# First attention: softmax rows transposed by VectorE in 32x32 blocks and a trip through DRAM, values a step later

## The chip, the core and the metric

The kernel runs on one core of a Trainium2 chip. A core has engines that work side by side, each through its own queue in order: TensorE (PE: matrix products and transposes), VectorE (DVE), ScalarE (ACT), GpSimd (POOL), and SyncE (SP), which only issues transfers (DMA). A transfer can also be issued from ScalarE's and GpSimd's queues. The engines share an on-chip memory, SBUF, of 128 partitions; TensorE writes to PSUM, which is used in banks of 128x512 float32. An instruction that waits for a semaphore holds back everything behind it on its own queue. The metric is the device time of one execution in microseconds (us).

## The reference

Four residual layers on x of 4 batches x 512 rows x 512 columns, float32, each behind a layer norm: a first attention, a feed-forward with ternary weights, a second attention with block-scaled weights, and the same feed-forward again. The change lies in the first attention and in work that runs beside it. That attention has 16 query heads over 4 key/value heads of 128, and adds causal softmax attention with rotary positions to a gated linear attention:

```python
scores = jnp.einsum('bqhd,bkhd->bhqk', sq, sk) * scale
scores = jnp.where(causal[None, None], scores, jnp.finfo(scores.dtype).min)
attn = jax.nn.softmax(scores, axis=-1)
y = jnp.einsum('bhqk,bkhd->bqhd', attn, sv)
o = 0.5 * y + 0.5 * o_gla
return o.reshape(b, n, H * D) @ Wo
```

`o_gla` is a recurrence over the rows with decays from the keys. The kernel computes it by chunks of 128 rows: products within a chunk (`own`) plus a state carried from the chunks before.

## The kernel before

**Tiling.** A group is one batch and one key/value head with its four query heads; there are 16 groups. Each has four chunks of 128 query rows, so 64 chunks. For chunk c of its group the scores reach over the c+1 chunks of keys up to its own, so their width is 128, 256, 384 or 512.

**The loop** in `first_attention_gentle` (from L518) runs over steps n, one chunk a step, and is pipelined over chunks by hand: a step works on the later parts of an early chunk and the early parts of a later one. The parts of a chunk are methods of `Chunk`:

- A projects its queries (L181 through `project`) and copies them to `q_t` (ScalarE, L430).
- B makes `qd`, softmax over the head dimension times a decay (L328 to L334: VectorE and ScalarE), and `qr`, the rotation (L319 and L322 on VectorE, the swapped half `sw` on GpSimd, L321).
- C transposes `qr` and `qd` on TensorE (L340) through a PSUM bank `tp`.
- own makes the chunk's part of the linear attention, masked by `until` (L448, L450).
- D(h) takes the scores of one head (TensorE, L456), adds the mask, takes the maximum (L459), exponentials with their sum (ScalarE, L462), reciprocal (L463) and the division (VectorE, L464). The result is `pr`, with query rows on the partitions.
- E(j) transposes key chunk j of the four heads' `pr` on TensorE (L472), four transposes to a bank, and takes the bank to SBUF as `wts`: for the chunk's own keys with `own` added (VectorE, L475), else by a copy on ScalarE (L477).
- F multiplies the values with `wts`, and the carried state with `qdT` (L484, L486), and halves the sum (`oT`, L488).
- G multiplies by Wo and adds to the residual (L181, L186).

In step n the chunk n+1 runs own and D, chunk n runs E between these and then F, chunk n-1 runs G, chunk n+2 runs C, chunk n+3 A and B. `part` prepares the next group: project, gates, decays (the running sum of the gates by a product with `until_r`, halves `gatehi` and `gatelo`), transposes of `kr` and `kd`, states.

**Beside it** two generators advance once a step. `quantise` makes the ternary weights of the feed-forward and stores them to DRAM as `blocks`. `prepare` multiplies codes by scales of the second attention's weights for 64 slices: five loads from SP a slice (L274, L276), a product on GpSimd (L290), a rounding copy on ScalarE (L281), a comparison on VectorE that counts inexact entries (L282), a store from SP to `exact` (L283).

**What sets the order.** The kernel's program order is the start of it; a scheduler then places instructions on each engine's queue by their dependences, except that those wrapped in `in_place` keep their order among each other. Buffers by tag (`bufs`) and PSUM banks (mm 2, sc 3, tp 2, pv 1) set what must wait for a reader.

**Feed-forward.** `feed_forward` keeps 11 weight blocks in SBUF (`block`, L252), in pools that take the place of the attention's. Block 0 is loaded into the pool `base` during the first attention (step 58) and serves both feed-forwards.

Of the kernel before, what the change touches and what calls it, by code (L numbers as in the profile page):

```python
# [19 lines left out]
P = 128  # L20
# [4 lines left out]
HG = 4  # L25
# [49 lines left out]
def hybrid_block(ctx: ExitStack, tc: tile.TileContext, a: dict, out: bass.AP):  # L75
# [186 lines left out]
    def prepare(pool):  # L262
# [5 lines left out]
        def fetch(i):  # L268
            g, n, k = slices[i]
            name = ("wq", "wk", "wv", "wo")[n]  # L270
            codes, scales = a[f"{name}_codes"], a[f"{name}_scales"]
            r, cols = (g * NK + k, slice(0, C)) if n == 3 else (k, slice(g * HG * D, (g + 1) * HG * D))
            w, sc = tiles[i] = [pool.tile([P, C], F32, tag=x, name=x) for x in ("codes", "scales")]
            in_place(nc.sync.dma_start(w, codes[r * P : (r + 1) * P, cols]))  # L274
            for q in range(4):
                in_place(nc.sync.dma_start(sc[q * 32 : (q + 1) * 32], scales[r * 4 + q, cols].partition_broadcast(32)))  # L276

        def rounded(i):
            g, n, k = slices[i]
            w, to = tiles.pop(i)  # L280
            in_place(nc.scalar.copy(to.bitcast(F32R), w))  # L281
            in_place(nc.vector.scalar_tensor_tensor(w, w, 1.0, to, ALU.mult, ALU.not_equal, accum_out=inexact[:, i : i + 1]))  # L282
            in_place(nc.sync.dma_start(exact[g, n, :, k, :], to))  # L283

        for i in range(-2, len(slices)):
            if i >= 0:
                rounded(i)
            if 0 <= i + 1 < len(slices):
                w, sc = tiles[i + 1]
                in_place(nc.gpsimd.tensor_tensor(w, w, sc, ALU.mult))  # L290
            if i + 2 < len(slices):
                fetch(i + 2)
# [3 lines left out]
    def first_attention_gentle(base, extra):  # L296

# [3 lines left out]
        with ExitStack() as st:  # L301
# [6 lines left out]
            until = one.tile([P, P], F32, tag="until", name="until")  # L308
            nc.scalar.dma_start(until, a["sums"][:, PREFIX, :])
            until_r = one.tile([P, P], F32R, tag="until_r", name="until_r")  # L310
            nc.scalar.copy(until_r, until)
# [38 lines left out]
            class Group:  # L350
# [33 lines left out]
                def decays(self):  # L384
# [4 lines left out]
                    project(dec.rearrange("p c d -> p (c d)"), lambda i: until_r, lambda i: halves[i].rearrange("p c d -> p (c d)"), 2)  # L389
# [7 lines left out]
                    self.kr = one.tile([P, NC, D], F32, tag="kr", name="kr")  # L397
# [24 lines left out]
            class Chunk:  # L422
# [9 lines left out]
                def B(self):  # L432
# [3 lines left out]
                    self.qr = two.tile([P, HG, D], F32, tag="qr", name="qr")  # L436
                    rotate(self.qr, self.q_t, turn[:, c : c + 1, 0:1, :], turn[:, c : c + 1, 1:3, :])

                def C(self):
                    self.qrT = two.tile([P, HG, P], F32, tag="qrT", name="qrT")  # L440
                    transposed(self.qrT, self.qr, nc.scalar.copy)
                    self.qdT = two.tile([P, HG, P], F32, tag="qdT", name="qdT", bufs=3)
                    transposed(self.qdT, self.qd, nc.scalar.copy)

                def own(self):
# [4 lines left out]
                    nc.vector.tensor_tensor(self.own_, sc, until.unsqueeze(1).to_broadcast([P, HG, P]), ALU.mult)  # L450
                    self.prs, self.wts = [], []

                def D(self, h):
                    c, width = self.c, (self.c + 1) * P
                    sc = bank("sc", [P, width])
                    nc.tensor.matmul(sc, lhsT=self.qrT[:, h, :], rhs=self.k.krT[:, :width], start=True, stop=True)  # L456
                    nc.vector.tensor_tensor(sc[:, c * P :], sc[:, c * P :], causal, ALU.add)
                    nm = two.tile([P, 1], F32, tag="nm", name="nm", bufs=4)
                    nc.vector.tensor_reduce(nm, sc, AX.X, ALU.max, negate=True)  # L459
                    pr = two.tile([P, S], F32, tag="pr", name="pr", bufs=7)[:, :width]  # L460
                    den = two.tile([P, 1], F32, tag="den", name="den", bufs=4)
                    nc.scalar.activation(pr, sc, AF.Exp, bias=nm, accum_out=den)  # L462
                    nc.vector.reciprocal(den, den)  # L463
                    nc.vector.tensor_scalar(pr, pr, den, None, ALU.mult)  # L464
                    self.prs.append(pr)

                def E(self, j):
                    if j > self.c:
                        return
                    tp = bank("tp", [P, HG, P])  # L470
                    for h in range(HG):
                        nc.tensor.transpose(tp[:, h, :], self.prs[h][:, j * P : (j + 1) * P], ident)  # L472
                    w = two.tile([P, HG, P], F32, tag="wts", name="wts", bufs=5)
                    if j == self.c:
                        nc.vector.tensor_tensor(w, self.own_, tp, ALU.add)  # L475
                    else:
                        nc.scalar.copy(w, tp)  # L477
                    self.wts.append(w)

                def F(self):  # L480
                    c = self.c
                    acc = bank("pv", [P, HG, P])
                    if c:
                        nc.tensor.matmul(acc, lhsT=self.k.state[:, c - 1, :], rhs=self.qdT, start=True, stop=False)  # L484
                    for j in range(c + 1):
                        nc.tensor.matmul(acc, lhsT=self.k.v_t[:, j, :], rhs=self.wts[j], start=j == c == 0, stop=j == c)  # L486
# [31 lines left out]
            for n in range(-7, last + 1):  # L518
# [4 lines left out]
                if p == 3 and (m + 1) % KV == 0 and (m + 1) // KV < B:  # L523
                    normalise((m + 1) // KV)
                part(m, p, 0)
                w, x, y, z = (at(i) for i in range(4))
                if n == -6:
                    nc.scalar.dma_start(turn, a["turn"])
                if x:
                    x.own()  # L530
                if w:
                    w.E(0)
                if x:
                    x.D(0)
                if w:
                    w.E(1)
                if z and n > -2:
                    z.A()
                if w:
                    w.E(2)  # L540
                if x:
                    x.D(1)
                if w:
                    w.E(3)
# [4 lines left out]
                if y:  # L549
                    y.C()  # L550
                if x:
                    x.D(3)
                part(m, p, 1)
# [567 lines left out]
```

## Time and profile before

Times are those of three runs: 2556.14, 2558.22 and 2559.29 us, median 2558.22. The profile is one further execution.

| what | value |
|---|---|
| the profiled execution | 2560.28 us |
| its span, first to last instruction | 2558.5 us |
| granted TensorE clock, mean | 0.998 |
| busy over the span: PE / DVE / ACT / POOL | 2523.9 / 1676.9 / 1140.8 / 248.4 us |
| first attention | to 1127 us |
| first feed-forward | 1127 us to about 1380 |
| second attention | about 1380 to 2306 us |
| last feed-forward | from 2306 us |
| moved by DMA | 248.88 MB, mean 97 GB/s |

A row of the groups reads: line, engine, operation, output<-input, the shapes, how many, then busy us and mean ns of one, then the idle time of the engine just before them and what ended it. Busy us counts overlapped time once, so with pipelined matrix products the mean times the count is more than the busy time. A float32 product of 128x512 counts as two MATMUL instructions; a transpose as one. In the chain of waits each piece begins where the one before it ended, so its lengths add up to the span. Bounds of stages come from the chain; the stretches of the busy table were cut by hand.

### The profile page before, as it was taken

Reading aid. Unit: us, or ns where it says so; the run is one execution under the profiler, and the core shown is the slowest. Engines: PE = TensorE matmul, PEld = TensorE weight load, DVE = VectorE, ACT = ScalarE, POOL = GpSimd, SP = SyncE. Lnnn points to the kernel's source line nnn. Section 1 sums busy time; section 2 is a strip of 40 time slices with the busy share of each in tenths; the row PEclk is TensorE's granted clock in tenths of the full one; section 3 lists DMA queues with packets and bytes.
Section 4 is the critical chain, followed back from the end, with each engine's and each line's share of the span. In section 5 each row is a group of like instructions: output and inputs, shape, how many; then the busy total and the mean of one; then the engine's idle time right before and its main releaser. Section 6 shows DMA issues by size and latency. Waiting matters only on the chain.

```text
span 2558.5 us, 29656 instructions
## 1 busy us (share of the span) xinstructions
PE 2523.9 (99%) x9448; PEld 1633.4 (64%) x9448; DVE 1676.9 (66%) x3858; ACT 1140.8 (45%) x2901; POOL 248.4 (10%) x263
## 2 busy tenths in 40 slices
PE   7999999999999999999999999999999999999999
PEld 5555555555555555568887666666666666657887
DVE  6888777888788878754445666666766666664332
ACT  4555555555555555542223444444444444432222
POOL 2121112112221121200001000000000000000000
PEclk9999999999999999999999999999999999999999
DMA  4344433443343332250003334353444434333000
GB/s 125 91 128 131 129 101 115 145 135 96 103 128 111 101 114 66 83 184 23 1 1 102 95 94 124 94 142 91 124 108 111 124 93 124 94 68 136 17 17 22
DMA packets 159045, 248.88 MB, mean 97 GB/s; under 512 B 33952, under 2 KB 61984, under 8 KB 154784
## 3 DMA queue, kind: packets, MB, share of 16 engines
q1 hardware_dynamic: 157584, 245.50, 33.4%
q8 instruction: 77, 1.26, 0.2%
q10 hardware_dynamic: 1296, 1.39, 0.2%
q14 instruction: 88, 0.72, 0.1%
HBM read 150.03 MB, written 29.62 MB: 70 GB/s over the span
## 4 chain that ended last, share of the span: by engine, by line
PE 90%; DVE 6%; DMA 2%; SPq 1%; issue 1%; ACT 0%; POOL 0%; ACTq 0%; DVEq 0%
PE mm L181 43%; PE sc L181 12%; PE sc L821 8%; PE sc L456 5%; PE pv L486 4%; PE tp L855 4%; PE pv L855 4%; PE tp L472 3%; PE tp L340 2%; PE sc L448 2%; PE pv L484 1%; PE tp L160 1%; SPq L848 1%; DVE qd L334 1%; DVE qr L319 1%
## 5 line engine op out<-in xcount | busy, mean ns | idle before, releaser
L826 ACT ACTIVATE pr<-sc,nm 128x512 f32<-128x512 f32 x256 | 175.9, 687 | 322.4 <-DVE nm L823 277.6
L181 PE MATMUL sc<-xnhi,block 128*128 128x512 f32 x704 | 278.7, 396 | 2.5 <-DMA block<-blocks 2.5
L181 PE MATMUL sc<-xnlo,block 128*128 128x512 f32 x704 | 275.6, 392 | 0.0
L821 PE MATMUL sc<-kT,qT 128*128 128x512 f32 x512 | 262.2, 594 | 0.0
L181 PE MATMUL mm<-xnhi,w 128*128 128x512 f32 x512 | 254.5, 497 | 0.0
L181 PE MATMUL mm<-wq,xnT 128*128 128x512 f32 x512 | 232.2, 595 | 0.0
L181 PE MATMUL mm<-wo,oT 128*128 128x512 f32 x512 | 231.4, 593 | 0.0
L823 DVE TENSOR_REDUCE nm<-sc 128x1 f32<-128x512 f32 x256 | 175.1, 684 | 82.0 <-PE sc L821 79.6
L462 ACT ACTIVATE pr<-sc,nm 128x128 f32<-128x128 f32 (+3 forms) x256 | 133.9, 523 | 162.7 <-DVE nm L459 157.7
L181 PE MATMUL mm<-xnlo,w 128*128 128x512 f32 x512 | 206.0, 402 | 0.0
L843 DVE STREAM_TRANSPOSE turned<-pr 128x512 f32<-128x512 f32 x256 | 173.5, 696 | 33.4 <-ACT pr L833 30.0
L833 ACT ACTIVATE pr<-pr,den 128x512 f32<-128x512 f32 x192 | 138.6, 722 | 79.3 <-DVE den L831 79.1
L456 PE MATMUL sc<-krT,qrT 128*128 128x512 f32 (+3 forms) x512 | 172.3, 434 | 0.0
L181 PEld LDWEIGHTS mm<-wo,oT 128*128 128x128 f32 x512 | 96.7, 190 | 118.0 <-issue 117.7
L321 POOL TENSOR_TENSOR sw<-q_t,turn 128x256 f32<-128x256 f32 x128 | 94.7, 760 | 676.5 <-ACT q_t L430 616.6
L1022 DVE TENSOR_TENSOR hT<-hT,sc 128x512 f32<-128x512 f32 x88 | 60.5, 687 | 141.0 <-PE sc L181 137.9
L181 PEld LDWEIGHTS mm<-wq,xnT 128*128 128x128 f32 x512 | 94.1, 192 | 91.4 <-issue 90.1
L181 PEld LDWEIGHTS sc<-xnhi,block 128*128 128x128 f32 x704 | 132.8, 189 | 30.7 <-issue 3.6
L181 PEld LDWEIGHTS sc<-xnlo,block 128*128 128x128 f32 x704 | 133.0, 189 | 27.3 <-issue 0.5
L486 PE MATMUL pv<-wts,v_t 128*128 128x512 f32 x320 | 147.9, 593 | 0.0
L821 PEld LDWEIGHTS sc<-kT,qT 128*128 128x128 f32 x512 | 95.7, 189 | 80.5 <-issue 63.1
L186 DVE TENSOR_TENSOR x<-x,mm 128x512 f32<-128x512 f32 x128 | 87.4, 684 | 78.6 <-PE mm L181 76.9
(143 smaller groups left out, 4968.0 us busy)
## 6 DMA issues: line engine op xcount, KB each, us to landing
prT<-turned SPq DMA_DIRECT2D x1024, 64.0 KB, 2.0
w<-exact SPq DMA_DIRECT2D x32, 1024.0 KB, 5.4
wq<-in_Wq SPq DMA_DIRECT2D x16, 1024.0 KB, 5.3
wo<-in_Wo SPq DMA_DIRECT2D x16, 1024.0 KB, 5.8
exact<-scales SPq DMA_DIRECT2D x64, 256.0 KB, 3.1
block<-blocks SPq DMA_DIRECT2D x21, 512.0 KB, 7.8
w<-in_w3T SPq DMA_DIRECT2D x22, 256.0 KB, 4.7
block<-blocks SPq DMA_DIRECT2D x21, 256.0 KB, 7.8
```

The lines of the kernel that those rows point to most:

```text
L181: nc.tensor.matmul(acc, lhsT=lhs(k), rhs=rhs(k), start=k == 0, stop=k == n - 1)
L186: nc.vector.tensor_tensor(xs[b * NC + c], xs[b * NC + c], y, ALU.add)
L321: nc.gpsimd.tensor_tensor(sw[:, :, i, :], s4[:, :, 1 - i, :], sin[:, :, i, :].to_broadcast([P, n, D // 2]), ALU.mult)
L456: nc.tensor.matmul(sc, lhsT=self.qrT[:, h, :], rhs=self.k.krT[:, :width], start=True, stop=True)
L462: nc.scalar.activation(pr, sc, AF.Exp, bias=nm, accum_out=den)
L486: nc.tensor.matmul(acc, lhsT=self.k.v_t[:, j, :], rhs=self.wts[j], start=j == c == 0, stop=j == c)
L821: nc.tensor.matmul(sc, lhsT=qTs[u][:, i * P : (i + 1) * P], rhs=kTs[u], start=True, stop=True)
L823: nc.vector.tensor_reduce(nm, sc, AX.X, ALU.max, negate=True)
L826: nc.scalar.activation(pr, sc, AF.Exp, bias=nm, accum_out=den)
L833: nc.scalar.mul(pr, pr, den)
L843: nc.vector.transpose(turns[u][:, :, i, :], pr.rearrange("p (q k) -> p q k", q=4))
L855: nc.tensor.matmul(accs[u].rearrange("p (n t) -> p n t", t=32), lhsT=v_ts[m, j][:, h * D : (h + 1) * D], rhs=prTs[u].rearrange("p a i (k t ...
```

## The change

Softmax rows no longer go through TensorE. D divides on ScalarE, and VectorE transposes the result in 32x32 blocks into one tile `turned` for the four heads; after the last head one transfer stores it to DRAM (`passed`), and E becomes four loads, one for each 32 partitions of `prT`, which bring the blocks to their places. So that this gives a whole transpose, the keys of the scores are taken in an order with the block index outermost (the rearranged `krT`), and the mask is read in the same order.

```diff
-    nc.tensor.matmul(sc, lhsT=self.qrT[:, h, :], rhs=self.k.krT[:, :width], start=True, stop=True)
+    nc.tensor.matmul(sc.rearrange("p q (k j) -> p q k j", j=32), lhsT=self.qrT[:, h, :], rhs=self.k.krT.rearrange("p (k q j) -> p q k j", q=4, j=32)[:, :, :n, :], start=True, stop=True)
...
     nc.vector.reciprocal(den, den)
-    nc.vector.tensor_scalar(pr, pr, den, None, ALU.mult)
-    self.prs.append(pr)
+    nc.scalar.mul(pr, pr, den)
+    nc.vector.transpose(self.turned.rearrange("p (q h x) -> p q h x", q=4, h=HG)[:, :, h, :], pr.rearrange("p (q x) -> p q x", q=4))
+    if h == HG - 1:
+        self.passed = dram.tile([P, 4 * HG * P], F32, tag="passed", name="passed", bufs=3)[:, : 4 * HG * 32 * n]
+        in_place(nc.sync.dma_start(self.passed, self.turned))
...
-    tp = bank("tp", [P, HG, P])
-    for h in range(HG):
-        nc.tensor.transpose(tp[:, h, :], self.prs[h][:, j * P : (j + 1) * P], ident)
-    w = two.tile([P, HG, P], F32, tag="wts", name="wts", bufs=5)
-    if j == self.c:
-        nc.vector.tensor_tensor(w, self.own_, tp, ALU.add)
-    else:
-        nc.scalar.copy(w, tp)
+    prT = two.tile([P, HG * P * (3 + self.c % 2)], F32, tag=f"prT{self.c % 2}", name="prT", bufs=1)[:, : 4 * HG * 32 * n]
+    for q in range(4):
+        in_place(nc.sync.dma_start(prT[32 * q : 32 * (q + 1)].rearrange("j (a x) -> j a x", a=4), self.passed.rearrange("(a j) (q x) -> q j a x", a=4, q=4)[q]))
+    self.wts = prT.rearrange("p (a h k t) -> p h a k t", a=4, h=HG, t=32)
```

F adds `own` to the last key chunk of `prT` on VectorE and multiplies from views of `prT`:

```diff
+    w = self.wts[:, :, :, c, :]
+    nc.vector.tensor_tensor(w, w, self.own_.rearrange("p h (a t) -> p h a t", a=4), ALU.add)
...
-        nc.tensor.matmul(acc, lhsT=self.k.v_t[:, j, :], rhs=self.wts[j], start=j == c == 0, stop=j == c)
+        nc.tensor.matmul(acc.rearrange("p h (a t) -> p h a t", a=4), lhsT=self.k.v_t[:, j, :], rhs=self.wts[:, :, :, j, :], start=j == c == 0, stop=j == c)
```

The loop runs one step further. F and G of a chunk come one step later, own a step later, C moves from late in the step to its start:

```diff
-            for n in range(-7, last + 1):
+            for n in range(-7, last + 2):
...
+                u, v, w, x, y, z = (at(i) for i in range(-2, 4))
+                if n >= -1:
+                    next(prepared, None)
+                if w:
+                    w.E()
                 part(m, p, 0)
...
+                if y:
+                    y.C()
                 if x:
                     x.D(0)
                 if z and n > -2:
                     z.A()
                 if x:
                     x.D(1)
+                if v:
+                    v.F()
+                if n >= -1:
+                    next(prepared, None)
                 if z:
                     z.B()
                 if x:
                     x.D(2)
+                if w:
+                    w.own()
...
+                part(m, p, 1)
+                if u:
+                    u.G()
+                if x:
+                    x.D(3)
```

`prepare` advances twice a step; its transfers are issued by GpSimd, and the inexact entries are found by a subtraction on GpSimd and an absolute sum on ScalarE in place of VectorE's comparison:

```diff
-            in_place(nc.sync.dma_start(w, codes[r * P : (r + 1) * P, cols]))
+            in_place(nc.gpsimd.dma_start(w, codes[r * P : (r + 1) * P, cols]))
             for q in range(4):
-                in_place(nc.sync.dma_start(sc[q * 32 : (q + 1) * 32], scales[r * 4 + q, cols].partition_broadcast(32)))
+                in_place(nc.gpsimd.dma_start(sc[q * 32 : (q + 1) * 32], scales[r * 4 + q, cols].partition_broadcast(32)))
...
+            in_place(nc.gpsimd.tensor_tensor(w, w, to, ALU.mult))
             in_place(nc.scalar.copy(to.bitcast(F32R), w))
-            in_place(nc.vector.scalar_tensor_tensor(w, w, 1.0, to, ALU.mult, ALU.not_equal, accum_out=inexact[:, i : i + 1]))
-            in_place(nc.sync.dma_start(exact[g, n, :, k, :], to))
+            in_place(nc.gpsimd.tensor_tensor(w, w, to, ALU.subtract))
+            in_place(nc.scalar.activation(w, w, AF.Abs, accum_out=inexact[:, i : i + 1]))
+            in_place(nc.gpsimd.dma_start(exact[g, n, :, k, :], to))
```

To fit in SBUF some tiles share or lose buffers: `kr` takes the tag of `gate`, `qr` has one buffer in place of two, `pr` three in place of seven, `qdT` four in place of three; `until` is kept once, in the rounded type, and filled by GpSimd at step -6. Block 0 of the feed-forward is no longer kept in `base`:

```diff
-        early = ahead(50, 0)
-        early.setdefault(58, []).extend(lambda f=f: heads.append(block((base, base), f)) for f in range(1))
-        first_attention_gentle(base, early)
+        first_attention_gentle(base, ahead(50, 0))
...
-            ws = ws + [block(pools, f) for f in range(len(ws), NF)]
+            ws = [block(pools, f) for f in range(NF)]
```

## The prediction

> **What bounds the kernel now.** I read the busy times by stage first, because the page's line 1 averages over four stages.
>
> ```profile
> core 0: us, PE busy (x) PEld busy (x) DVE busy (x) ACT busy (x) POOL busy (x), PEclk, DMA share, GB/s
> ...
> 256.00:384.00 128.00, 127.93 (x467) 73.77 (x466) 100.66 (x256) 67.80 (x210) 25.14 (x26) 1.00 0.37 115
> ...
> 640.00:768.00 128.00, 127.08 (x482) 73.69 (x481) 106.27 (x299) 68.36 (x210) 27.77 (x30) 1.00 0.38 115
> ```
>
> In the first attention (0 to 1127 us) TensorE is busy over 99% of each stretch at full clock; VectorE is at about 81%, ScalarE at 53%, GpSimd at 20%. TensorE sets the time, so an edit gains what it takes from TensorE's queue and loses what TensorE then waits for. Next the groups by form between 128 and 1024 us (columns: line, engine, operation, output<-input, shapes, count | busy us, mean ns | idle before).
>
> ```profile
> L472 PE MATMUL tp<-ident,pr 128*128 128x128 f32 x520 | 78.0, 273 | 0.0
> L321 POOL TENSOR_TENSOR sw<-q_t,turn 128x256 f32<-128x256 f32 x103 | 76.1, 759 | 554.4 <-ACT q_t L430 494.5 <-DVE pr L464 47.8 <-DVE mv L132 12.1
> L290 POOL TENSOR_TENSOR codes<-codes,scales 128x512 f32<-128x512 f32 x52 | 75.1, 1444 | 99.5 <-DMA scales<-in_wv_scales 19.8 <-DVE pr L464 19.1 <-DMA scales<-in_wo_scales 15.4
> L319 DVE TENSOR_TENSOR qr<-q_t,turn 128x512 f32<-128x512 f32 x52 | 49.8, 957 | 0.0
> L477 ACT COPY wts<-tp 128x512 f32<-128x512 f32 x78 | 44.7, 580 | 22.2 <-PE tp L472 22.1
> L282 DVE SCALAR_TENSOR_TENSOR codes<-codes,scales 128x512 f32<-128x512 f32 x52 | 37.0, 711 | 0.0
> L475 DVE TENSOR_TENSOR wts<-own,tp 128x512 f32<-128x512 f32 x52 | 35.3, 679 | 22.8 <-PE tp L472 22.8
> L464 DVE TENSOR_SCALAR pr<-pr,den 128x384 f32<-128x384 f32 x52 | 27.2, 522 | 1.3
> L464 DVE TENSOR_SCALAR pr<-pr,den 128x512 f32<-128x512 f32 x52 | 24.8, 477 | 0.5
> L319 DVE TENSOR_TENSOR kr<-k_t,turn 128x512 f32<-128x512 f32 x13 | 8.7, 666 | 0.0
> ```
>
> The transposes of L472 are what the change removes. Their mean of 273 ns is not their price, since they are pipelined; the chain of waits gives the time between them. The same view gives the stage boundaries:
>
> ```profile
> 1091.57 0.44 PE tp L472 x4
> ...
> 1127.65 3.91 DMA block<-blocks
> ```
> ```profile
> 2306.48 3.76 DMA block<-blocks
> ```
>
> So 0.109 us per transpose. The x16 runs of projections in that chain stand at 220.99, 288.77 and 356.75 us: 67.9 us per group of four chunks, 17.0 us per step of the loop.
>
> **The change part by part.**
>
> *TensorE.* Per group E made (1+2+3+4) x 4 = 40 transposes; over 16 groups 640 x 0.109 = **69.5 us leave the bound engine**, and a step falls from 17.0 to 15.9 us. No product is added. The products now read their moving operand in runs of 32; the second attention does that already (L855, mean 593 ns, as L486 has with whole rows), so I cost it at nothing.
>
> *VectorE.* Gone: L464 in four widths (296+383+522+477 ns) x 64 = 107; L475, 64 x 0.68 = 43; the check of L282 with its 81 ns accumulator read, 64 x 0.79 = 51; together 201 us. Added: 256 block transposes and 64 additions of `own`. For the transposes two rows of the second attention stand near:
>
> ```profile
> L843 DVE STREAM_TRANSPOSE turned<-pr 128x512 f32<-128x512 f32 x256 | 173.5, 696 | 33.4 <-ACT pr L833 30.0 <-DMA prT<-turned 3.0
> L833 ACT ACTIVATE pr<-pr,den 128x512 f32<-128x512 f32 x192 | 138.6, 722 | 79.3 <-DVE den L831 79.1
> ```
>
> L459 over the same widths takes 284/410/551/680 ns; a transpose at 696 is 16 more, so (300+426+567+696) x 64 = 127. The addition has both inputs in SBUF: between 666 ns (the `kr` row) and 957 (the `qr` row); I take 0.8, 51 us. Net -23 us: it stays near 83% of a shorter stage.
>
> *ScalarE.* Gone: 96 copies x 0.58 = 56. Added: the division, 722 ns at 512 and less by the steps of L462 (360/476/578/678), so (404+520+622+722) x 64 = 145; and `Abs` with its accumulator read, near 629+193 ns (L380, L396), 53. Net +142 us: from about 53% to 70%. Hidden as long as no TensorE wait ends on it.
>
> *GpSimd.* Today a step holds 2 x 0.76 + 0.4 (`sw` of q, and of k spread) + 1.44 = 3.4 us. Added: a subtraction (1.44, as L290) and six DMA issues. No row shows an issue from GpSimd. From below: an issue by SP, 0.44 us (four `scales` took 1.77 us in the timeline). From above: the Trainium skill (DMA: Bandwidth & Descriptors, Anatomy of one DMA) counts about 2.0 us fixed for a whole DMA of this kind, of which the issue can be only a part. I take 1.0 us, the first-byte latency that the same page gives under Latency and other measured facts, where it puts it down to this issuing work; an estimate. The step then has 10.8 us of 15.9 (7.4 to 16.8 by the two ends).
>
> Here a rule speaks against the change. SBUF — State Buffer (Who interferes with whom) says that VectorE with two SBUF inputs, and GpSimd reading SBUF, lock one another out for a whole instruction. The row first:
>
> ```profile
> 388.42 1.27 POOL L290 TENSOR_TENSOR codes<-codes,scales 128x512 f32<-128x512 f32 x1
> ...
> 388.60 1.64 DVE L319 TENSOR_TENSOR qr<-q_t,turn 128x512 f32<-128x512 f32 x1
> ```
>
> L319 took 1.64 us beside GpSimd against 0.67 for the `kr` form: the trace agrees. By the rule at its worst each of the 64 subtractions costs VectorE its whole 1.44, 92 us, and VectorE would stand at 92%. By the rows, the excess of L319 and L322 (957 and 882 over 666) is 64 x 0.51 = 32 us for 212 us of GpSimd arithmetic; 92 us more adds 14. I take 14. The same section warns that descriptors written by GpSimd wait for VectorE in a two-port mode; L464, whose 512 form is faster than its 384 form and so may run in one, leaves VectorE, which weakens that.
>
> *The DMA path.* A chunk's `turned` goes to DRAM and back before F. Rows near:
>
> ```profile
> w<-exact SPq DMA_DIRECT2D x32, 1024.0 KB, 5.4
> ...
> exact<-scales SPq DMA_DIRECT2D x64, 256.0 KB, 3.1
> ```
>
> At most 1 MB out (5.4), four issues of 0.44 to 0.59, 256 KB in (3 to 5): 12 us. Before it VectorE finishes the last head (4 to 8 us). In the built order the TensorE work from the last score of a chunk to the product needing its weights is about 24 us, so it is hidden with 4 us or more to spare. On SP the store waits for VectorE, and the loads behind it for its landing; `wq` (5.3 us) and `wo` (5.8) stand behind such waits. In the order `wq` comes before the loads of its step and has a step to land; `wo` is issued when its last reader ends and has 14 us. Both hidden; a late one costs its excess, once a group.
>
> *C earlier, F later.* In the built order the TensorE work between a chunk's q projection (A) and the transposes of its q (C) falls from about 17 us to 9.3-12.4. The chain between is q_t 0.59, maximum 0.68, four exponentials with reads 2.3, reciprocal 0.17, four L334 1.5: 5.3 us, and some 7 us as VectorE's queue stands. Slack shrinks to about 2 us at the tightest step. `sw`, which `qr` needs, stands on GpSimd behind the issues; in one step of four (second chunk, values late) the chain subtraction, six issues, product ends about 2.4 us after q_t is there. Also the projection of k to the gates' product has 4.3 us of TensorE work in place of 6.9, for a chain of 0.27+1.09+0.63+0.63+0.68+0.62 = 3.9 plus five handovers. These two are **what is late next**: I put 1.1 us a group on the two together at each of 16 groups, 18 us (5 to 35).
>
> *Block 0.* It was resident at both feed-forwards and gave 16 products (3.6 us) while block 1 came. Now block 0 itself is loaded only when the last product has freed its place: the two DMA lines above (3.91, 3.76), bare. Less the 0.5 waited today at the first, **+7.4 us**.
>
> *Ends.* The extra step at the end of the loop leaves the last round trip less cover: about 16 us of path against 19 us of TensorE work in the order; +3 (0 to 8). At the start ScalarE no longer waits for `until` (11.30 us), worth up to 2 us, but the gates' product stands with less ahead of it: +1.
>
> **Sum**: -69.5 + 7.4 + 3 + 1 + 18 = -40 on a span of 2558.5: 2518. The profiled execution took 2560.3 and the runs' median is 2558.2, so the span stands for the median: **2518 us**.
>
> **The rivals.**
> 1. *All slack holds* (no late q, no late gates): 2500. For it: by the waits of TensorE up to 1150 us no cause but the first layer norm (12.2 us) holds it for more than 2.0 us in all. Against: those distances are cut by a third. Chance 0.12.
> 2. *GpSimd becomes the bound* (the other side). At 2 us an issue its step is 16.8 us, with about 1 us of waiting for ScalarE's copy before the subtraction 17.8, and `sw` then holds `qr`: 64 x 0.8 = +51, with the ends +11: **2620**. It decides from 1.85 us an issue, (15.9 - 4.8)/6; slower than now from about 1.9. Against: 4.8 us of the step is arithmetic, and the price I took leaves 5 us free. Chance 0.17.
> 3. *VectorE's queue becomes the bound*: a transpose behind a reciprocal waits for ScalarE's division. In the order about half stand directly behind it, 8 x 0.7 = 5.5 us a group on 53 of 63.6: enough room. If all wait and the port lock is at its worst, 53 + 11 + 5 = 69 us a group, 1 more than now; halfway, 66, the gain shrinks to about 12-20 us: 2542. Chance 0.13.
> 4. *The weights come late*: a miss of 5 us a group, 80 us, on the main sum: 2590. Chance 0.05.
>
> **How the numbers follow.** The forecast itself has 0.53, with a range of its own of 2503 to 2540. Two runs of this kernel differ by about 3 us (2556.14 to 2559.29), so 0.2%, 5 us, is no change. Faster: 0.53 + 0.12 + most of rival 3, 0.10 = 0.75. Same: 0.04. Slower: 0.17 + 0.05 less the edge = 0.21. Below 2490 nothing leads; to leave out no more than 0.2 the range goes up to 2582.
>
> **What would show it.** No `tp<-pr` rows before 1100 us; TensorE at 96% or more in the stage and groups 64 to 65 us apart; waits of PE ending on `qr`, `qd` or `gatehi`, a few tenths to 2 us each; bare waits on block 0 near 4 us twice; GpSimd's issues near 1 us and `sw` late one step in four. I am wrong if `sw` is late in every step, if PE waits on `prT`, or if groups stay 68 us apart.

## The result, and the profile after

The changed kernel takes 2646.45 us (median of 4 runs, 2641.98 to 2649.09) against 2558.34 before (4 runs, 2556.14 to 2559.29): a ratio of 1.0344, interval 1.0326 to 1.0362. It is slower by 88 us; the forecast was 2518. The profiled execution has a span of 2643.5 us and a mean granted clock of 0.981 (before: 2558.5 and 0.998).

The windows of the changed kernel, the same two stretches as before and then the whole first attention:

```profile
core 0: us, PE busy (x) PEld busy (x) DVE busy (x) ACT busy (x) POOL busy (x), PEclk, DMA share, GB/s
256.00:384.00 128.00, 121.23 (x393) 65.77 (x391) 101.35 (x242) 79.29 (x242) 58.03 (x78) 1.00 0.69 195
640.00:768.00 128.00, 116.84 (x365) 64.95 (x364) 96.16 (x225) 76.24 (x228) 52.83 (x74) 0.95 0.57 165
0.00:1206.92 1206.92, 1084.70 (x3470) 593.06 (x3470) 928.31 (x2245) 715.92 (x2137) 497.79 (x687) 0.96 0.59 172
```

No engine is the bound any more: in the two stretches TensorE fell from over 99% to 95% and 91%, VectorE is no fuller, ScalarE and GpSimd have room. The chain of waits gives the ends of the stages:

```profile
1206.92 3.58 DMA block<-blocks
...
2389.76 3.65 DMA block<-blocks
```

The first attention ends at 1206.92 us instead of 1127.65, 79.3 later; what follows takes 1436.6 us (2643.5 less 1206.92) instead of 1430.9. These 5.7 us are put down to block 0, and the loss lies in the first attention. The same window of the kernel before:

```profile
0.00:1127.65 1127.65, 1105.78 (x4088) 639.82 (x4089) 892.14 (x2359) 597.60 (x1846) 218.78 (x238) 1.00 0.37 111
```

TensorE is busy for 1084.70 us, against 1105.78 before: 21 less. It is idle for 122.2 us (1206.92 less 1084.70), against 21.9: 100 more. The two make the 79. What it waits for, from TensorE's waits in that stretch (line, releaser, us in total, times, longest), and below it the gates' wait in the kernel before:

```profile
PE mm L181 <- ACT gatehi L120: 57.4, 15, 6.2
PE tp L160 <- DVE xn L157: 24.2, 9, 8.5
PE mm L181 <- DVE x L186: 7.6, 8, 1.6
PE mm L181 <- ACT v_t L378: 7.0, 6, 1.8
...
PE pv L493 <- DVE prT L488: 2.3, 6, 0.6
```
```profile
PE mm L181 <- ACT gatehi L120: 2.0, 3, 1.2
```

The gates' product waits in 15 of the 16 groups, 3.8 us on average. The way through DRAM (`prT`) costs next to nothing. One such wait by windows of 2 us:

```profile
382.00:384.00 2.00, 0.37 (x1) 0.00 (x0) 1.06 (x3) 2.00 (x8) 1.42 (x3) 1.00 0.45 145
384.00:386.00 2.00, 0.00 (x0) 0.00 (x0) 1.85 (x3) 1.08 (x2) 2.00 (x3) 0.67 0.38 117
386.00:388.00 2.00, 0.47 (x1) 0.41 (x2) 1.91 (x3) 0.62 (x1) 2.00 (x5) 0.50 0.09 33
388.00:390.00 2.00, 2.00 (x9) 1.69 (x8) 1.96 (x5) 0.78 (x2) 0.25 (x1) 0.50 0.28 98
390.00:392.00 2.00, 2.00 (x8) 1.25 (x7) 1.27 (x5) 2.00 (x9) 0.00 (x0) 0.62 0.00 0
```

Read the first number behind the length (TensorE busy) against PEclk, the third from the end: some 2 us into the gap, which began at 382.4, the clock falls to half, and it is back only about 4 us after the work (by the shares 0.67 and 0.62 half clock runs from 384.7 to 391.5, 6.8 us). A gap is paid once as idle time and again as slow products. And the chain into that gap, from the timeline (start, us, engine, line, operation):

```profile
380.21 1.27 POOL L283 TENSOR_TENSOR codes<-codes,scales 128x512 f32<-128x512 f32 x1 [3.70 <-ACT scales L282]
...
381.51 0.63 ACT L284 ACTIVATE codes<-codes 128x512 f32<-128x512 f32 x1 [1.39 <-POOL codes L283]
...
382.81 0.25 ACT L377 COPY k_t<-mm 128x128 f32<-128x128 f32 x1
...
385.02 1.26 POOL L281 TENSOR_TENSOR codes<-codes,scales 128x512 f32<-128x512 f32 x1
385.14 1.69 DVE L387 SCALAR_TENSOR_TENSOR gate<-k_t,gate 128x512 f32<-128x512 f32 x1
...
387.54 0.79 PE L181 MATMUL mm<-gatehi,until 128*128 128x512 f32 x1 [5.17 <-ACT gatehi L120]
```

ScalarE stands for 1.39 us at `Abs`, waiting for GpSimd's subtraction; the copy of `k_t`, which begins the gates' chain, is queued behind it. Then VectorE's second gate operation takes 1.69 us beside GpSimd's product, where it took 678 ns on average before:

```profile
L382 DVE SCALAR_TENSOR_TENSOR gate<-k_t,gate 128x512 f32<-128x512 f32 x15 | 10.2, 678 | 0.0
```

Both delays come with the new preparation's work.

### The profile page after: what moved, and what is told of

It is laid out like the page before. It is cut to its first block, busy times and chain, and to the rows that moved or that the text cites. A ratio compares the mean times of both kernels' runs of the same rounds, so it can differ in the third digit from the quotient of the medians.

```text
span 2643.5 us, 29287 instructions
## 1 busy us (share of the span) xinstructions
PE 2502.8 (95%) x8808; PEld 1584.6 (60%) x8808; DVE 1708.6 (65%) x3730; ACT 1258.5 (48%) x3188; POOL 527.5 (20%) x712
## 3 DMA queue, kind: packets, MB, share of 16 engines
q10 hardware_dynamic: 1296, 1.39, 0.2%
## 4 chain that ended last, share of the span: by engine, by line
PE 70%; DVE 12%; ACT 6%; DMA 5%; POOL 3%; issue 3%; SPq 1%; ACTq 0%; DVEq 0%; POOLq 0%
PE mm L181 34%; PE sc L181 12%; PE sc L825 8%; PE tp L859 4%; PE pv L859 4%; PE pv L493 2%; PE sc L463 2%; PE tp L345 2%; DVE qd L339 1%; DMA exact<-scales 1%; ACT pr L472 1%; POOL codes L283 1%; DMA w<-in_w3T 1%; PE tp L160 1%; DVE turned L473 1%
## 5 line engine op out<-in xcount | busy, mean ns | idle before, releaser
L181 PE MATMUL mm<-wq,xnT 128*128 128x512 f32 x512 | 244.7, 619 | 1.7 <-DVE x L186 1.6
L181 PE MATMUL mm<-wo,oT 128*128 128x512 f32 x512 | 237.2, 603 | 4.5 <-DMA wo<-in_Wo 3.6
L472 ACT ACTIVATE pr<-pr,den 128x128 f32<-128x128 f32 (+3 forms) x256 | 142.8, 562 | 130.5 <-DVE den L471 129.3
L463 PE MATMUL sc<-krT,qrT 128*128 128x512 f32 (+3 forms) x512 | 181.7, 444 | 2.7 <-ACT pr L470 2.7
L181 PEld LDWEIGHTS mm<-wq,xnT 128*128 128x128 f32 x512 | 100.3, 202 | 109.8 <-issue 98.8
L139 POOL TENSOR_TENSOR rstd<-var,power 128x4 f32<-128x4 f32 (+1 forms) x19 | 17.6, 938 | 724.6 <-DVE var L137 723.0
L473 DVE STREAM_TRANSPOSE turned<-pr 128x128 f32<-128x128 f32 (+3 forms) x256 | 128.9, 506 | 49.8 <-ACT pr L472 46.9
L493 PE MATMUL pv<-prT,v_t 128*128 128x512 f32 x320 | 150.1, 596 | 3.1 <-DVE prT L488 2.3
```

Of the source, the lines that this page charges most:

```text
L181: nc.tensor.matmul(acc, lhsT=lhs(k), rhs=rhs(k), start=k == 0, stop=k == n - 1)
L463: nc.tensor.matmul(sc.rearrange("p q (k j) -> p q k j", j=32), lhsT=self.qrT[:, h, :], rhs=self.k.krT.rearrange("p (k q j) -> p q k j", q= ...
L472: nc.scalar.mul(pr, pr, den)
L473: nc.vector.transpose(self.turned.rearrange("p (q h x) -> p q h x", q=4, h=HG)[:, :, h, :], pr.rearrange("p (q x) -> p q x", q=4))
L493: nc.tensor.matmul(acc.rearrange("p h (a t) -> p h a t", a=4), lhsT=self.k.v_t[:, j, :], rhs=self.wts[:, :, :, j, :], start=j == c == 0, s ...
```

## The experiments

Three theories. **A**: the new order leaves too little TensorE work between the keys' projection and the gates' product. **B**: the preparation's arithmetic, now two GpSimd products and two ScalarE operations a slice, makes VectorE and ScalarE late. **C**: the queues of transfers do it, GpSimd's with the new preparation or SyncE's without it. The later runs add a fourth, **D**: VectorE's queue as a whole is late, so that a wait taken from one of its results goes to another. The kernel before stood at 2557 to 2559 us beside all of these.

**1. More distance for the gates (A).** In the changed kernel, the third and fourth part of the keys' group go behind the products with values:

```diff
+                if p < 2:
-                part(m, p, 0)
+                    part(m, p, 0)
...
                     v.F()
+                if p > 1:
+                    part(m, p, 0)
```

> The changed kernel with one thing moved: the gates' product (decays) and the transposes of k are placed behind F in their step, not at its start. In the built order TensorE then has about 12.5 us of work between the last projection of k and the gates' product, against 4.3 us. Theory A (the distance is too short: TensorE stands at the gates' product in every group for 3.8 us, and the clock is halved for some us after each of these gaps): the 54 us of waits on gatehi go, and most of the 51 us by which the same products took longer go with them; 2550 to 2575 us. Theory B (ScalarE's queue, where the copy of k stands behind the absolute sum that waits for GpSimd, delays everything; the gates' product is only where it shows first): the wait goes to the next consumer, kr/kd or qr/qd; 2610 to 2645. Theory C (VectorE is held by late loads of quantise on the busier DMA queues): as B, 2620 or more.

Measured 2607.24 us, 39 less than the changed kernel, 1.0189 [1.0159, 1.0218] of before. That is in the range of neither theory, 3 us short of B's. The gates' wait falls from 57.4 to 4.8 us, and others stand in its place, from TensorE's waits in this run:

```profile
PE tp L345 <- DVE qd L339: 22.4, 10, 3.5
PE tp L160 <- DVE xn L157: 13.1, 7, 9.1
PE sc L453 <- ACT pr L470: 12.5, 6, 4.8
PE pv L493 <- DVE prT L488: 11.6, 10, 2.6
```

A explains part of the loss. VectorE and ScalarE are late elsewhere too, as B says.

**2. Less of the new preparation (B).** First VectorE's comparison of the kernel before comes back in place of subtraction and `Abs`; then only the subtraction moves to VectorE, and `Abs` stays.

```diff
-            in_place(nc.gpsimd.tensor_tensor(w, w, to, ALU.subtract))
-            in_place(nc.scalar.activation(w, w, AF.Abs, accum_out=inexact[:, i : i + 1]))
+            in_place(nc.vector.scalar_tensor_tensor(w, w, 1.0, to, ALU.mult, ALU.not_equal, accum_out=inexact[:, i : i + 1]))
```

> The changed kernel with VectorE's comparison again in place of GpSimd's subtraction and ScalarE's absolute sum; the transfers of prepare stay on GpSimd's queue, and the order on TensorE stays as it was. Theory A: VectorE gets 51 us more work, ScalarE loses the 58 us in which it waited for GpSimd; the distance at the gates' product stays 4.3 us, so the waits on gatehi shrink by some 1 to 2 us a group only; 2600 to 2635. Theory B: ScalarE is free of the wait, the copy of k comes at once, the waits on gatehi fall under 1 us a group; 2560 to 2590. Theory C: no better than now, 2640 or more.

> The changed kernel, the preparation's subtraction moved from GpSimd to VectorE alone; ScalarE's Abs stays. VectorE then does as much as with the comparison that gave 2588 us, GpSimd 64 x 1.27 = 81 us less. Theory B1 (GpSimd's product is the harm, because VectorE stands still beside it): within 15 us of 2588, 2575 to 2605 us. Theory B2 (ScalarE's second operation and the wait of its queue for the subtraction is the harm): 2620 to 2650 us, as the changed kernel.

Measured 2588.23 (1.0114 [1.0083, 1.0146]) and 2596.67 us (1.0155 [1.0135, 1.0175]). VectorE was given an operation more in both, and both gained: 58 and 50 us. The gates' wait falls to 26.7 and 30.5 us in all, not under 1 us a group as theory B had it. So GpSimd's second product does the harm here (B1); `Abs` is worth the remaining 8, which two runs of each hardly tell from nothing.

**3. The new preparation in the kernel before.** Whole; then with VectorE's comparison (so GpSimd gains the transfers, and the product moves beside the rounding); then with the subtraction but with SyncE's transfers.

> The kernel before with prepare alone changed (transfers issued by GpSimd, subtraction and absolute sum, two advances a step); TensorE's transposes and the order of the loop stay. Theory A: the distances of before (6.9 us to the gates' product, some 17 us from A to C) cover it: 2555 to 2572. Theory B: ScalarE's wait for GpSimd delays this kernel too: 2590 to 2640. Theory C: the DMA traffic of turned is absent here, so no loss: 2555 to 2565.

> The kernel before, with the preparation's transfers issued by GpSimd and its work in two advances a step, but VectorE's comparison kept. The whole new preparation cost +61 us in this kernel. Theory B (GpSimd's second product and ScalarE's Abs do the harm): within 15 us of before, 2545 to 2575 us. Theory C (GpSimd's issues, 0.5 us each and six a step, hold up the rotations' products): 2590 us or more.

> The kernel before, with the preparation's GpSimd subtraction and ScalarE Abs in two advances a step, but with its transfers left on SyncE. Theory B: most of the +61 us, 2595 to 2630 us. Theory C: 2545 to 2580 us.

Measured 2620.53, 2590.48 and 2601.60 us: +61, +33 and +44. The first and the third are in theory B's range. The preparation does its harm without the new order of the first attention. The second run meets theory C's "2590 us or more" by its number, at the very edge. The way that C names isn't there: VectorE waited for `sw` for 0.8 us in all. Its gate rows show a cause that is not the transfers, first the kernel before, then this run:

```profile
L379 DVE SCALAR_TENSOR_TENSOR gate<-k_t 128x512 f32<-128x512 f32 x15 | 15.9, 1063 | 3.8 <-ACT k_t L372 3.8
```
```profile
L378 DVE SCALAR_TENSOR_TENSOR gate<-k_t 128x512 f32<-128x512 f32 x15 | 34.4, 2296 | 3.8 <-ACT k_t L371 3.8
```

The product of GpSimd now falls beside this first gate operation. How much of the 33 is the issues' stays open. In the whole version one such operation, from the timeline of that run:

```profile
321.81 3.41 DVE L379 SCALAR_TENSOR_TENSOR gate<-k_t 128x512 f32<-128x512 f32 x1
322.03 1.42 POOL L321 TENSOR_TENSOR sw<-k_t,turn 128x256 f32<-128x256 f32 x2
323.39 1.26 POOL L281 TENSOR_TENSOR codes<-codes,scales 128x512 f32<-128x512 f32 x1
```

VectorE's operation starts just ahead and ends at 325.22, behind all three GpSimd products: their 1.42 + 1.26 and its own 0.68 make 3.36 of the 3.41.

**4. SyncE's queue (C).** The changed kernel with the whole preparation of before, its transfers on SyncE; then also with the four loads of the transposed rows in the middle of the step.

> The changed kernel with prepare as before: transfers from SP, comparison on VectorE, one advance a step. All else, the transposes through DRAM among it, stays. Theory A: the distance stays short, so most of the loss stays: 2600 to 2640, unless the scheduler itself moves the gates' product. Theory B: ScalarE and GpSimd are free, 2550 to 2590. Theory C: SP now carries all loads behind the stores of turned that wait for VectorE, so it gets worse: over 2650.

> The changed kernel with the whole preparation of before (2702 us), and the four loads of the transposed rows moved from the start of the step to its middle, ahead of the products with values. Theory C (SyncE stands still at the four loads until the store before them has landed, and the preparation's loads are late behind it): 2600 to 2650 us. If the number of SyncE's transfers or the preparation's order does it and not the standing still: 2680 to 2710 us.

Measured 2702.11 (1.0559 [1.0529, 1.059]) and 2714.50 us (1.0607 [1.0576, 1.0638]). The first lies where theory C put it, the second just above the range that speaks against C's reason. As arranged here SyncE can't carry both: in the second run GpSimd's product waits 312 us for late scales, and leaving the transfers on SyncE is no way out. What holds SyncE up isn't settled. It is not the four loads: in the first run they waited 6.9 us in all for the store before them, and only when they were moved 77.4 us. SyncE's waits are spread over many tiles (a store behind `tern` first, 118.3 us in the first run, 84.9 in the second).

**5. No arithmetic at all.** Both products, `Abs` and the comparison are left out, so the second attention's weights are not the reference's; the transfers and the rounding stay. In the changed kernel; in the kernel before; and in the changed kernel with edit 1.

> The changed kernel without the preparation's arithmetic: both GpSimd products, ScalarE's Abs and the comparison are left out (the codes are rounded and stored as they come, the flags of inexactness stay zero), its transfers from GpSimd stay. GpSimd does 64 x 2.55 = 163 us less and VectorE the same as in the changed kernel. Theory B (GpSimd's products stretch VectorE, and that opens TensorE's gaps): TensorE's saving of 69.5 us shows, 2510 to 2550 us. Theory A (the short distances of the new order and the path through DRAM open the gaps by themselves): 2565 to 2610 us.

> The kernel before without the preparation's arithmetic: GpSimd's product and VectorE's comparison are left out, the transfers stay with SyncE. The control of the run above. Both theories: TensorE runs nearly without gaps in the kernel before, so no more than its 10 us of gaps can go, 2545 to 2560 us.

> The changed kernel without the preparation's arithmetic (2542 us; both products, Abs and comparison left out), and the third part of the keys' group placed behind the products with values. Theory A (what is left of the loss there, some 46 us, comes from the short distance between gates and their product): 2505 to 2530 us. Theory D (VectorE's queue as a whole is late, wherever the gates stand): 2535 to 2560 us, with the wait moved from the gates to the queries' transposes or the added own block.

Measured 2542.35 (0.9931 [0.9908, 0.9953]), 2551.52 (0.9972 [0.9961, 0.9982]) and 2524.60 us (0.9870 [0.9841, 0.9898]). These runs divide the loss. The arithmetic costs 104 us in the changed kernel (2646.45 less 2542.35) and 8 in the kernel before (2559.35 less 2551.52). Without it on both sides the new order gains 9 us (2551.52 to 2542.35), and with more distance for the gates 27 (to 2524.60, which theory A expected): less than the forecast's 40. GpSimd still issues the transfers here, and stands 149 us for the stores of its slices in the first of these runs, so its queue of transfers (C) is not what costs the 104. The windows of the first attention, with more distance, and before it without:

```profile
0.00:1085.73 1085.73, 1046.69 (x3470) 577.46 (x3470) 852.35 (x2246) 673.43 (x2009) 337.15 (x559) 0.99 0.66 191
```
```profile
0.00:1103.73 1103.73, 1049.87 (x3470) 578.18 (x3470) 860.80 (x2246) 671.12 (x2009) 332.14 (x559) 0.99 0.65 188
```

And the kernel before without the arithmetic:

```profile
0.00:1116.60 1116.60, 1098.09 (x4084) 639.07 (x4085) 814.60 (x2231) 596.57 (x1846) 131.88 (x174) 1.00 0.36 112
```

In the changed kernel without the arithmetic VectorE runs the same instructions as with it (x2246, one more to clear the flags, and x2245) and is busy for 860.80 us instead of 928.31: 67.5 us of the changed kernel's VectorE time is stretch beside GpSimd's products.

**6. The product on VectorE too.** Edit 2, and `nc.vector` in place of `nc.gpsimd` for the product `w * to`; and that product alone in the kernel before.

> The changed kernel with VectorE's comparison (2588 us), and the preparation's product on VectorE too: VectorE 64 x 0.68 = 44 us more, GpSimd 64 x 1.27 = 81 us less. Theory B (beside GpSimd's product VectorE stands still for about as long as it would take to do it): 2565 to 2595 us. If VectorE loses nothing beside GpSimd and is merely full: 2610 to 2640 us.

> The kernel before with the preparation's product moved from GpSimd to VectorE, nothing else. Theory B: TensorE has only 10 us of gaps there, so at most a few us go: 2550 to 2562 us. If VectorE were full beside a busier TensorE: 2565 to 2590 us.

Measured 2553.30 (10 runs, 2547.68 to 2559.75; 0.998 [0.9966, 0.9994]) and 2556.71 us (0.9995 [0.9988, 1.0002]). With all of the arithmetic on VectorE the changed kernel takes 93 us less than with it on GpSimd and ScalarE, below the range of theory B even, and VectorE is busy for 931.38 us against 928.31:

```profile
0.00:1118.30 1118.30, 1057.64 (x3470) 581.21 (x3470) 931.38 (x2437) 672.77 (x2009) 339.40 (x559) 0.99 0.65 186
```

The gate operations show the stretch go; first the changed kernel, then this one (groups by form; its numbers are a line lower):

```profile
L387 DVE SCALAR_TENSOR_TENSOR gate<-k_t,gate 128x512 f32<-128x512 f32 x15 | 18.8, 1254 | 1.8 <-ACT gate L386 0.3
L384 DVE SCALAR_TENSOR_TENSOR gate<-k_t 128x512 f32<-128x512 f32 x15 | 17.2, 1149 | 1.0 <-ACT k_t L377 1.0
```
```profile
L383 DVE SCALAR_TENSOR_TENSOR gate<-k_t 128x512 f32<-128x512 f32 x15 | 11.1, 738 | 1.0 <-ACT k_t L376 1.0
L386 DVE SCALAR_TENSOR_TENSOR gate<-k_t,gate 128x512 f32<-128x512 f32 x15 | 10.1, 675 | 1.1
```

In the kernel before, the product's move gives no change that the interval tells. Of the versions that do all of the arithmetic, the changed kernel with it on VectorE is the fastest: 0.2% under before.

**7. Combinations.** With VectorE's comparison: more distance (edits 1 and 2); GpSimd's product half a step ahead of its rounding; that product issued behind the first part of the keys' group; that and more distance. Last, comparison and product on VectorE, the product half a step ahead, and more distance.

> The changed kernel with both of the edits that gained alone: VectorE's comparison in place of GpSimd's subtraction and ScalarE's Abs (2588 us alone), and the third part of the keys' group placed behind the products with values (2607 us alone). Theory A (the short distance of the gates' product and the long chain of the preparation lose the same microseconds, since TensorE waits where the two meet): the gains overlap, 2545 to 2585 us. Theory B (the preparation's stretch of VectorE and the distance lose apart): the gains add, 2588 - 39 = 2549 us or below, 2525 to 2550 us, and the prediction's sum of -40 us would then be near for a kernel without both.

> The changed kernel with VectorE's comparison (2588 us) and, beside it, GpSimd's product of a slice half a step ahead of its rounding, so that product, rounding and comparison are no longer one chain in one advance. Theory B (the product's place beside VectorE's long operations matters, not the chain): 2575 to 2600 us. Theory B' (the chain holds the queues up): 2550 to 2575 us.

> The changed kernel with VectorE's comparison and the product ahead of its rounding (2575 us), where product and loads are now issued behind the first part of the keys' group and not ahead of it, so that no preparation stands between the gates and their product. Theory A with B: the gates' wait of 26 us falls below 12 us, 2545 to 2570 us. Theory D: 2565 to 2590 us.

> The run above with the third and fourth part of the keys' group behind the products with values as well. Theory A: no wait at the gates, 2535 to 2560 us. Theory D: no gain over the run above, since the queries' transposes and the added own block wait in its place.

> The changed kernel with the preparation's product and comparison both on VectorE, the product half a step ahead of its rounding, and the third part of the keys' group behind the products with values. The product on VectorE alone gave 2553 us, of which the gates' wait is 18 us; without the arithmetic the later third part gained 18 us (2542 to 2525). Theory A with B: 2525 to 2548 us, faster than both kernels. Theory D (VectorE's queue is full and the wait moves, as it did in the other two runs with the later part): 2548 to 2570 us.

Measured 2590.57, 2575.28 (7 runs, 2567.99 to 2589.79), 2580.92, 2576.84 and 2573.09 us. Distance gains nothing over edit 2 alone (2588.23), where both theories expected 2585 or less, and 4 us between the third and the fourth, as theory D had it. The product half a step ahead gives 13, at the edge between the two expectations: not settled. Issued later (the third run) it met the gates again: their second operation took 1146 ns, and their wait is 32.8 us, not below 12. The last is 20 us slower than the run of experiment 6, against theory A and 3 us above the range of D. Its gates wait only once, 3.8 us at the start; from 40 us on TensorE waits for the queries and others instead:

```profile
PE tp L346 <- DVE qd L340: 12.1, 10, 2.4
PE mm L181 <- DVE state L425: 10.9, 7, 2.2
PE pv L494 <- DVE prT L489: 9.6, 6, 2.6
PE sc L464 <- ACT pr L471: 7.6, 4, 3.3
```

Two edits went in together there, so which of them costs the 20 us isn't known. The waits move between results of VectorE, as theory D says; that its queue is the reason is not shown, since it is busy for 82% of the stage (928.02 of 1135.06 us).

## Why the prediction was wrong, point by point

**The step that failed is the pricing of the preparation's arithmetic.** The prediction costed GpSimd's subtraction as 14 us of VectorE's busy time, spread over a VectorE with room, and ScalarE's work as "hidden as long as no TensorE wait ends on it"; in the sum both are nothing. The arithmetic costs 104 us in the new order against 8 in the old (experiment 5). Of these, 58 went with the subtraction and `Abs` (experiment 2), and 35 more with the product (2588.23 to 2553.30, experiment 6), which was there before but now meets other work. Two things were wrong in the pricing.

- *The size.* VectorE's stretch was read as 32 us for all of GpSimd's arithmetic in the kernel before, `sw` among it, plus 14 for the subtraction at the same rate. In the kernel before the product alone makes 27: 892.14 less 814.60 without arithmetic, less the 51 us of the comparison. In the changed kernel the two products make 67.5. The excess grew by 41, not 14. The Trainium skill, SBUF — State Buffer (Who interferes with whom), says that the two engines lock each other out for a whole instruction where VectorE takes two inputs from SBUF and GpSimd reads it; the row of 3.41 us in experiment 3 agrees, and this operation waited for three products, not one. The prediction's worst by that rule was 92 us of growth, and the measured 41 lies between. Averaging over `sw` and the product was the mistake: at the product's own rate a second one would add 27 (an estimate from the same figures), and the other 14 us are put down to what the products now stand beside.
- *The kind.* Busy time was the wrong unit. In experiment 6 VectorE is as busy as in the changed kernel and the time is 93 us less. The gates' rows there, and the chain into the gap, show where the stretch and the waits of ScalarE and GpSimd for each other fell: in the gates' chain, with TensorE's work behind it.

**The terms of the sum.**

| Term | Forecast, us | Measured, us |
|---|---|---|
| TensorE's transposes | -69.5 | -51, by TensorE's busy time with the arithmetic left out on both sides and more distance in the changed kernel (1046.69 against 1098.09; the clock is 0.99 against 1.00) |
| Distances, "what is late next" | +18 (5 to 35) | +18 without the arithmetic (2542.35 to 2524.60), +39 with it (experiment 1) |
| Arithmetic of the preparation | 0 | +104 in place of 8 |
| TensorE's clock | 0 | +38 of busy time (1084.70 against 1046.69), inside the rows above |
| Block 0 | +7.4 | +5.7, all that follows the first attention |
| Ends of the loop | +4 | +5, TensorE's idle time in the first 40 us (14.4 against 12.0) and the last 20 (2.6 against 0) |

Without the arithmetic on either side and with more distance, the change gains 27 us, where the forecast without its 18 for the distances has 58. The sum was thus too good there too: TensorE lost 51 us of work and not 69.5, and was idle for 20 us more (39.0 against 18.5). What makes these two differences isn't shown in full.

The distances were well sized for what they are alone; with late engines they cost twice that. Block 0 was put too high because TensorE had already waited 2.0 us for a block at the last feed-forward. The gates' product was named as what is late next, with the right chain, but at 1.1 us a group together with the queries, where the gates alone waited 3.8 us, and without the half clock that such a gap brings. The rule stands in the Trainium skill, TensorE: Matmul & The Clock Gate, Part 1: The HAM clock gate, which puts the window at about 3.4 us and lets the clock fall after an idle one. This trace agrees on the length: the half clock lasted 6.8 us, two such windows. It differs on the start: the clock fell 2.3 us into a gap of 5.2, before a whole window had been idle. The costs overlap, so they don't add to 88.

**What held.** The transposes of VectorE (302 to 707 ns), the division (402 to 721) and the added `own` (782 ns against 0.8) came as costed. The way through DRAM is hidden: TensorE waited 2.3 us behind `prT`. `sw` was late for 12 of 64 chunks (VectorE waited 22.5 us for it), near the "one step in four". The bare wait of near 4 us on block 0 came once, 3.8 us, not twice: at the last feed-forward it was 0.5. Groups stand 72.6 us apart (358.50 to 431.14), more than the 68 that the prediction named among its three signs of being wrong; the other two, `sw` late in every step and waits on `prT`, did not come.

**The rivals.** Full slack (2500) fell. GpSimd as the bound fell: its issues took 0.50 to 0.60 us, not 1.85, and it is busy for 41% of the stage, 58% with its issues (64 slices at 0.60, 0.54 and four times 0.50 us); it does its harm at that share. VectorE's queue (2542) had a right mechanism, the lock, and the wrong size and place: it put it on the transposes that wait for the division. Late weights fell: 3.6 us for `wo`. The slow side was thus argued from a price of issues, while the cost lay in GpSimd's arithmetic, which stood in the same paragraph.

**What stays open.** Which share of the 104 us is VectorE's lock and which is ScalarE's and GpSimd's queues standing for each other: experiment 2 leaves 8 us for `Abs`, but the subtraction's move takes both a lock and a wait away. And what the GpSimd issues cost in the kernel before, beside the product's place (experiment 3).

## What to carry to other kernels

An operation that is moved off a busy engine onto an idle one is not free if the two stretch each other: price it at each place where it can fall beside the first engine's long operations, not as a mean over the stage. To find what takes the last slack from a chain, follow that chain through every queue that the change adds to. A TensorE gap like the one of 5.2 us here is to be costed with the half-clock time behind it. Leaving the side work out on both sides of a change (experiment 5) tells whether the change or its company costs the time.

## What the runs showed of the hardware

A VectorE operation with two inputs in SBUF stood still for three GpSimd products in a row, 3.41 us, not for one. Over the 14 versions of the changed kernel here, with the same products, TensorE's busy time in the first attention grows with its idle time, from 1046.69 us at 39.0 idle over 1084.70 at 122.2 to 1109.08 at 167.7 (the second run of experiment 4): between these ends about half a us more for each us of gap. And a transfer's issue by GpSimd took longer than the same one by SyncE in the kernel before, but well under the 1.0 us of the prediction: 0.50 us for the `scales` against 0.41, 0.54 for the `codes` against some 0.35, 0.60 for the stores against 0.38.
